# Four graph layers on 32 graphs: two broadcast sums moved from VectorE to GpSimd, one scaling moved from VectorE into ScalarE's PSUM evacuation

## The chip, the cores and the metric

The kernel runs on one core of one Trainium2 chip. The metric is device time in microseconds (us) of one execution; a run here is one such time. The engines are named as in the profile: PE (TensorE matmul) and PEld (its weight loads), DVE (VectorE), ACT (ScalarE), POOL (GpSimd), and SP (SyncE), whose queue issues all DMAs of this kernel.

## What is computed

Input is x of 32 graphs with 512 nodes and 256 features each, and adj, a 512 x 512 integer adjacency per graph. Four layers follow each other, each of the form

```
x = layernorm(x + layer(x, adj))
```

Layer 0 is graph attention with four heads of 64, a residual and a layernorm per head. Layer 1 is graph attention with a relu score and an elu. Layer 2 is a transformer block: eight heads of 32 over the symmetric adjacency, then a feed-forward of 1024. Layer 3, the one that the change touches most, is graph attention with one head:

```python
Wh = einsum('bnf,of->bno', h, W)
e = (Wh @ a1)[:, :, None] + (Wh @ a2)[:, None, :]
e = where(e > 0, e, 0.2 * e)
e = where(adj == 0, NEG_INF, e)
h_prime = einsum('bij,bjo->bio', softmax(e, axis=2), Wh)
```

## The kernel before

A graph's 512 nodes lie as R = 4 blocks of 128 rows on the partitions, so a tile of x is 128 x 4 x 256 fp32. K = 2 is the number of 128-wide pieces of the 256 features. Everything stays in SBUF from the load of a graph to its output.

**Exponentials without a score matrix.** In layers 0, 1 and 3 the exponential of a leaky relu of f + g is a maximum of two products. So the kernel takes exponentials of the two score columns alone (lines 665 to 667 in layer 3), brings one of them along the free axis with PE transposes into a bank gp and an ACT copy gb (line 345), and makes each masked weight tile pt with one DVE operation, max then multiply by the edges (line 393). What depends on the key alone, exp(0.2 g) in layer 3, is a factor on the key's row of values. In layer 3 it is written into column 256 of h (line 667) and multiplied onto the 256 value columns by DVE (line 668). The matmul of pt with 257 columns of h then gives numerators and the denominator at once.

**Projection.** `project` makes h from the transposed input: per row block two matmul steps into one PSUM bank, then one ACT copy of all columns into SBUF (line 333). Layers 0, 1 and 3 use it. In layer 3 the banks come from a pool of two that is shared with the feed-forward. Column 256 holds the query score f, column 257 the key score g.

**Two sums with a broadcast vector.** Layer 0 ends with a head layernorm scaled by gamma; its shift beta is added to the residual x earlier, off that path (line 437). In layer 2, `attended` makes y = x + bo for its own residual (line 599) and then adds the shift of the block's last layernorm to x (line 600), which is read again only at the end of the feed-forward (line 655). All three, 599, 600 and 437, are DVE operations on 128 x 1024 elements with the vector broadcast over the four row blocks.

**Layernorm.** `layernorm` takes statistics per row block on DVE (lines 266 and 267), adds eps (line 269), raises to the power -1/2 on POOL (line 270), multiplies by the mean (line 271) and applies scale and bias on ACT, one activation per row block (line 275). `head_layernorm` has a power on POOL of its own (line 297). Otherwise POOL sets a column of ones in layer 1 (line 466).

**Order of work.** The layers are generators; each yield carries a due time from the table PLACES plus PERIOD times the graph's number, and a merge by due time interleaves about three and a half graphs. PE's order is this merge, fixed by a manual schedule. On the other engines a scheduler of the tile framework sets the order when the program is built. Each engine runs its own queue in order and waits on semaphores.

At the end of each softmax part the row sums' reciprocals go to a tile rd, and a last check over them and over the adjacency decides whether a slower general program runs; with these inputs it does not.

## Time and profile before

| what | value |
|---|---|
| median of 3 runs | 3910.18 us (3910.09 to 3910.24) |
| profiled execution, its own time | 3906.41 us |
| its span, first to last instruction | 3904.6 us |
| mean granted TensorE clock | 0.983 |
| one graph in steady state | 116.77 us |
| DVE L437, 128 x 1024 | 1.22 us x32 |
| DVE L600, 128 x 1024 | 1.22 us x32 |
| DVE L668, 128 x 1024 | 1.22 us x32 |
| ACT L333 on h3p, 128 x 258 | 0.37 us x128 |

An engine's busy time is the sum over its instructions. Matmuls are pipelined and their ends are modelled. In a line of the timeline the numbers are start and length in us, then the engine, the line, the operation, output and inputs, and in brackets the idle time before it and what ended it. PE's matmuls all show line 102, so they are told apart by the tile that they write: h3p is layer 3's projection, gp the transposed exponentials, cp the attention of layer 2 times its values, xt1p and xt3p the transposed inputs of layers 1 and 3. L556 multiplies layer 2's exponentials pr by the edges.

### The profile page before, as it was taken

Reading aid. Unit: us, or ns where it says so; the run is one execution under the profiler, and the core shown is the slowest. Engines: PE = TensorE matmul, PEld = TensorE weight load, DVE = VectorE, ACT = ScalarE, POOL = GpSimd, SP = SyncE. Lnnn points to the kernel's source line nnn. Section 1 sums busy time; section 2 is a strip of 40 time slices with the busy share of each in tenths; the row PEclk is TensorE's granted clock in tenths of the full one; section 3 lists DMA queues with packets and bytes.
Section 4 is the critical chain, followed back from the end, with each engine's and each line's share of the span. In section 5 each row is a group of like instructions: output and inputs, shape, how many; then the busy total and the mean of one; then the engine's idle time right before and its main releaser. Section 6 shows DMA issues by size and latency. Waiting matters only on the chain.

```text
span 3904.6 us, 53602 instructions
## 1 busy us (share of the span) xinstructions
PE 3753.3 (96%) x19238; PEld 2824.5 (72%) x19238; DVE 2674.8 (69%) x5594; ACT 1926.2 (49%) x4257; POOL 346.9 (9%) x266
## 2 busy tenths in 40 slices
PE   5899999999999999999999999999999999999996
PEld 4577777777777777777777777777777777777764
DVE  4667676677677677677677677677777677777653
ACT  2444455444455544455544455545555544555442
POOL 0000010000010001010001010001010001010000
PEclk6899999999999999999999999999999999999998
DMA  3222222222222222222222222222222222221120
GB/s 106 77 73 65 72 58 67 71 76 67 70 60 65 71 76 69 68 62 63 71 76 71 66 63 64 69 76 71 66 65 65 65 76 74 63 67 58 49 54 12
DMA packets 180431, 261.20 MB, mean 67 GB/s; under 512 B 36800, under 2 KB 72768, under 8 KB 180160
## 3 DMA queue, kind: packets, MB, share of 16 engines
q1 hardware_dynamic: 180160, 257.71, 23.1%
q8 instruction: 155, 2.54, 0.3%
q14 instruction: 116, 0.95, 0.1%
HBM read 106.57 MB, written 16.78 MB: 32 GB/s over the span
## 4 chain that ended last, share of the span: by engine, by line
PE 60%; DVE 14%; issue 8%; ACT 5%; POOL 5%; POOLq 0%; ACTq 0%
PE o L102 16%; PE f1p L102 7%; PE f2p L102 6%; PE qkp L102 5%; PE cp L102 5%; DVE pr L556 4%; ACT y L275 4%; POOL rs L270 3%; PE h3p L102 3%; PE s L102 3%; PE h1p L102 3%; PE wop L102 3%; POOL st L297 2%; PE gp L102 2%; PE vp L102 2%
## 5 line engine op out<-in xcount | busy, mean ns | idle before, releaser
L556 DVE TENSOR_TENSOR pr<-pr,a 128x1024 f32<-128x1024 f32 x384 | 459.1, 1216 | 319.3 <-ACT pr L553 319.2
L275 ACT ACTIVATE y<-y,rs 128x256 f32<-128x256 f32 x768 | 398.4, 589 | 438.2 <-DVE rs L271 438.2
L393 DVE SCALAR_TENSOR_TENSOR pt<-gb,ex,at 128x512 f32<-128x512 f32 x768 | 530.6, 744 | 77.6 <-ACT gb L345 77.6
L553 ACT ACTIVATE pr<-s 128x512 f32<-128x512 f32 x1024 | 545.2, 613 | 7.4 <-PE s L102 7.3
L102 PEld LDWEIGHTS o<-hv,pt 128*128 128x128 f32 x4096 | 508.4, 199 | 23.7 <-issue 8.4
L102 PE MATMUL o<-hv,pt 128*128 128x65 f32 x4096 | 502.7, 280 | 9.7 <-DVE pt L393 9.7
L102 PE MATMUL f2p<-wf,ft 128*128 128x256 f32 x2048 | 491.6, 383 | 12.3 <-ACT ft L638 12.2
L102 PE MATMUL cp<-pr,v 128*64 128x512 f32 x2048 | 474.9, 600 | 17.8 <-DVE pr L556 17.1
L102 PE MATMUL f1p<-yt,wf 128*128 128x256 f32 x2048 | 488.9, 381 | 0.3 <-DVE yt L302 0.3
L102 PE MATMUL o<-h,pt 128*128 128x257 f32 x2048 | 482.8, 383 | 3.7 <-DVE pt L393 3.7
L102 PEld LDWEIGHTS o<-h,pt 128*128 128x128 f32 x2048 | 381.5, 190 | 96.0 <-issue 40.6
L270 POOL TENSOR_TENSOR rs<-rs,mhalf 128x4 f32<-128x4 f32 x192 | 246.2, 1282 | 2118.8 <-DVE rs L269 1826.0
L638 ACT ACTIVATE ft<-f1p,cols 128x256 f32<-128x256 f32 x512 | 215.2, 474 | 442.2 <-PE f1p L102 442.2
L102 PEld LDWEIGHTS f2p<-wf,ft 128*128 128x128 f32 x2048 | 380.1, 191 | 69.5 <-ACT ft L638 17.1
L102 PEld LDWEIGHTS f1p<-yt,wf 128*128 128x128 f32 x2048 | 385.3, 191 | 54.5 <-DVE yt L302 0.8
L102 PE MATMUL s<-qk 128*128 128x512 f32 x1024 | 395.1, 481 | 1.6 <-ACT pr L553 1.6
L102 PEld LDWEIGHTS cp<-pr,v 128*64 128x64 f32 x2048 | 133.0, 136 | 286.0 <-issue 194.2
L266 DVE BATCH_NORM_STATS2 bn<-y 128x6 f32<-128x256 f32 x768 | 294.6, 411 | 4.5
L102 PEld LDWEIGHTS s<-qk 128*128 128x128 f32 x1024 | 187.8, 190 | 99.3 <-issue 40.6
L102 PE MATMUL qkp<-xt,wqkv 128*128 128x512 f32 x512 | 231.3, 594 | 0.0
L345 ACT COPY gb<-gp 128x512 f32<-128x512 f32 x192 | 111.5, 581 | 219.4 <-PE gp L102 219.4
L428 DVE RECIPROCAL rd<-o 128x4 f32<-128x4 f32 x128 | 23.4, 183 | 272.7 <-PE o L102 272.7
(134 smaller groups left out, 4582.5 us busy)
## 6 DMA issues: line engine op xcount, KB each, us to landing
qk<-hi SPq DMA_DIRECT2D x1024, 64.0 KB, 2.0
qk<-lo SPq DMA_DIRECT2D x1024, 64.0 KB, 2.0
adjt<-in_adjt SPq DMA_DIRECT2D x64, 512.0 KB, 3.5
adj<-in_adj SPq DMA_DIRECT2D x64, 512.0 KB, 3.6
xt<-in_xt SPq DMA_DIRECT2D x32, 512.0 KB, 3.4
x<-in_x SPq DMA_DIRECT2D x32, 512.0 KB, 4.7
out<-y SPq DMA_DIRECT2D x32, 512.0 KB, 3.0
wf<-in_w1t SPq DMA_DIRECT2D x1, 1024.0 KB, 7.6
```

Of the source, the lines that this page charges most:

```text
L102: latest[0] = what(*args, **kwargs).ins.name
L266: nc.vector.bn_stats(st[:, r, :], y[:, r, :])
L270: nc.gpsimd.tensor_tensor(rs[:, 1, :], rs[:, 0, :], mhalf[:, :R], op=ALU.pow)
L275: nc.scalar.activation(y[:, r, :], y[:, r, :], AF.Identity, bias=rs[:, 2, r : r + 1], scale=rs[:, 1, r : r + 1],)
L297: nc.gpsimd.tensor_tensor(st[:, 2, :], st[:, 1, :], mhalf[:, :G], op=ALU.pow)
L345: nc.scalar.copy(g, p)
L393: nc.vector.scalar_tensor_tensor(t, g, f, edges, op0=ALU.max, op1=ALU.mult)
L428: nc.vector.reciprocal(rdh, o[:, :, HO:])
L553: nc.scalar.activation(t[:, i, :], s, AF.Exp, scale=QSCALE)
L556: nc.vector.tensor_mul(t, t, edges)
L638: nc.scalar.activation(ft[:, f, :], p[:, f, :], AF.Relu, bias=bf1[:, ff + f : ff + f + 1])
```

## The change

Three operations leave DVE. The sums of lines 437 and 600 are issued on POOL instead, with the same operands. The scaling of line 668 goes: `project` gets an optional slope, and for layer 3 each row block leaves PSUM in three ACT instructions instead of one: a copy of the two score columns, an exponential of the key score with scale 0.2 into a small tile f, and a scaled pass of the 256 value columns with f as the factor per partition.

```diff
-    def project(xt, w, cols, name):
+    def project(xt, w, cols, name, slope=None):
...
-            nc.scalar.copy(h[:, r, :], p[:, :cols])
+            if slope is None:
+                nc.scalar.copy(h[:, r, :], p[:, :cols])
+            else:
+                nc.scalar.copy(h[:, r, cols - 2 :], p[:, cols - 2 : cols])
+                f = buf([P, 1], "f", "f", 4)
+                nc.scalar.activation(f, p[:, cols - 1 : cols], AF.Exp, scale=slope)
+                nc.scalar.activation(h[:, r, : cols - 2], p[:, : cols - 2], AF.Identity, scale=f)
         return h
...
-        nc.vector.tensor_add(x, x, all_rows(bet0))
+        nc.gpsimd.tensor_add(x, x, all_rows(bet0))
...
-        nc.vector.tensor_add(x, x, all_rows(ln2b))
+        nc.gpsimd.tensor_add(x, x, all_rows(ln2b))
...
-        h = yield from project(xt, w3g, D + 2, "h3")
+        h = yield from project(xt, w3g, D + 2, "h3", 0.2)
...
-        nc.vector.tensor_mul(h[:, :, :D], h[:, :, :D], f.to_broadcast([P, R, D]))
```

In the built program PE's instructions keep their order. On POOL each graph's sum of line 600 stands directly behind the power of layer 0's closing layernorm of a later graph, and the sum of line 437 directly behind that. On ACT the scheduler places one of layer 3's exponentials (line 665) between the small pieces and the large piece of the last row block, and puts a layernorm's four passes (line 275) ahead of the first of layer 2's hi (line 504).

## The prediction

> **What bounds the kernel now.** The page's first part comes first:

> ```profile
> PE 3753.3 (96%) x19238; PEld 2824.5 (72%) x19238; DVE 2674.8 (69%) x5594; ACT 1926.2 (49%) x4257; POOL 346.9 (9%) x266
> ```

> TensorE is busy nearly always; the change takes nothing from it. The long pieces of the chain of waits repeat every 116.77 us (one graph), so I read one such stretch in the table of busy time by window:

> ```profile
> 1740.54:1857.30 116.76, 115.08 (x602) 86.94 (x601) 83.07 (x175) 60.02 (x133) 10.46 (x8) 1.00 0.24 69
> ```

> PE is busy 115.08 of 116.76 us at full clock, so all that any change off PE can win is 1.68 us a graph. PE's waits in that stretch (who waited for whom, total, times, longest):

> ```profile
> PE gp L102 <- ACT ex L665: 0.7, 1, 0.7
> PE xt3p L102 <- ACT y L275: 0.5, 3, 0.2
> PE cp L102 <- DVE pr L556: 0.5, 1, 0.5
> ```

> Two of these three places are touched. In the timeline of PE (start, length, work, idle before):

> ```profile
> 1794.46 1.94 PE L102 MATMUL cp<-pr,v 128*64 128x512 f32 x8
> 1796.89 1.94 PE L102 MATMUL cp<-pr,v 128*64 128x512 f32 x8 [0.49 <-DVE pr L556]
> ...
> 1844.78 2.01 PE L102 MATMUL h3p<-w3g,xt 128*128 128x258 f32 x8
> 1847.49 0.65 PE L102 MATMUL gp<-ident,ex 128*128 128x128 f32 x4 [0.70 <-ACT ex L665]
> ```

> DVE ahead of the first stall:

> ```profile
> 1793.45 1.19 DVE L599 TENSOR_TENSOR y<-y,bo_b 128x1024 f32<-128x1024 f32 x1
> 1795.54 0.16 DVE L271 SCALAR_TENSOR_TENSOR rs<-mv,rs 128x4 f32<-128x4 f32 x1 [0.90 <-POOL rs L270]
> 1795.62 1.22 DVE L556 TENSOR_TENSOR pr<-pr,a 128x1024 f32<-128x1024 f32 x1
> 1796.75 1.22 DVE L600 TENSOR_TENSOR y<-y,ln2b_b 128x1024 f32<-128x1024 f32 x1
> ```

> POOL there, and at a power of the same size with DVE idle:

> ```profile
> 1793.52 1.99 POOL L270 TENSOR_TENSOR rs<-rs,mhalf 128x4 f32<-128x4 f32 x1 [8.84 <-DVE rs L269]
> ...
> 1823.44 1.01 POOL L270 TENSOR_TENSOR rs<-rs,mhalf 128x4 f32<-128x4 f32 x1 [14.55 <-DVE rs L269]
> ```

> What to see: a DVE chain without slack, from layer 0's last output through L298, L440, L441, the statistics, the power on POOL (L270) and L271 to L556, ends in PE. L600 stands behind it and holds nobody. The power took 1.99 us instead of 1.01: it ended 0.87 us after L599 did (1794.64).

> ACT at the second stall:

> ```profile
> 1844.38 0.62 ACT L333 COPY h<-h3p 128x258 f32<-128x258 f32 x2
> 1844.89 0.58 ACT L345 COPY gb<-gp 128x512 f32<-128x512 f32 x1
> 1845.96 0.37 ACT L333 COPY h<-h3p 128x258 f32<-128x258 f32 x1 [0.48 <-PE h3p L102]
> 1846.83 0.37 ACT L333 COPY h<-h3p 128x258 f32<-128x258 f32 x1 [0.50 <-PE h3p L102]
> 1847.23 0.21 ACT L665 ACTIVATE ex<-h 128x4 f32<-128x4 f32 x1
> ```

> PE stands from the last h3p until the exponentials that gp transposes.

> [...] (1) [...] The trace agrees in one direction: powers that meet such a DVE operation end 0.87 us after it (L599 at 1794.64, power 1795.51; L384 at 1841.19, power 1842.06; L393 at 1858.87, power 1859.74). The other direction, DVE held by POOL, it does not show. (2) [...] The trace agrees at the start: memsets begin 0.06 us before the one ahead ends.

> **The change part by part.** The built order of PE's instructions is the same as before; DVE loses 96 instructions, POOL gains 64, ACT gains 256.

> *DVE's share.* L437, L600 and L668 leave DVE: 3 x 1.22 = 3.65 us a graph, 117 us in all. Worth nothing in time: at 1806.17 (L437) DVE next waits for ACT's softmax at 1809.34; L600 is followed by idle time until 1799.89; L668 (1849.43) lets layer 3's masks start 1.13 us sooner, but PE wants them at 1853.68 and did not wait. What covers this is PE's own work; without it, at the very end, L668 waited for by o3 saves below 0.1 us, since the gb copy ends then too (3885.69 against 3885.79).

> *L437 on POOL.* It waits for x's DMA: issued 1799.35, landing 4.7 us later, 1804.05. It then meets two L556 (1803.90 to 1806.26); whoever wins, all are done by 1808.7, and the next cp starts at 1811.21. Behind it on POOL stand the memset L466 (1808.79) and a power at 1823.44. Cost 0 (-0 to +0.5 a graph). Once, at 77.4 us, it follows a power directly: up to 2.3.

> *L600 on POOL.* In POOL's order it stands directly behind the power of 1793.52, ahead of L437. Its waits (L599, layer 1's output and its transposes) are over at 1794.64, so by (2) it starts with the power's end, 1795.5, as L271 is only being released (1795.54). L271 has two SBUF inputs, L556 too. [...] Its length is not in the trace: [...] and I take 2.3 with the handover (2.2 to 2.6). Then L271 starts at 1797.8, L556 ends 1799.1, and the second half of cp starts 2.3 us later; ACT's y (L275) and xt1p's transposes move with it (y ready 1800.1, PE there 1801.1: no more). PE's order is fixed and nothing after is ahead of PE, so the stall is not won back: **+2.3 us a graph** (0 if L271 wins, 2.6 at most). New waits for POOL in L441 and L655 come some 30 us after their sums: 0.

> *ACT's evacuation.* For each of four row blocks, one copy (0.37 us, next one 0.26 later) becomes a copy of 2 columns, an exponential of 1 and a scaled activation of 256, which waits for the exponential. Prices: [...] the exponential 0.19 (L667's row: 0.21 from SBUF); the scaled one 0.46 as L476. First block: 1844.38, 1844.45, 1844.67 to 1845.13, so its bank comes free 0.38 us later, and PE's third block starts at 1845.16. The second ends 1845.78, gb 1846.26 (its masks start 1846.46 on DVE: hidden). The third block is ready at 1846.31, its last piece ends 1847.09; the fourth at 1847.2: small copy to 1847.36, then, as the built order has it, L665's exponential ahead of the large piece, 1847.59. gp starts 1847.62 instead of 1847.49: **+0.13 us a graph** (-0.2 if the three pipeline, +0.5 if the exponential takes 0.3).

> *Reordering.* ACT now does a layernorm (four L275) ahead of the first hi (L504), 2.9 us later. SP's 32 copies for the first head pairs then start at 1745.9, not 1743.0, and end by 1769; the scores that need them come at 1775, and SP stands from 1770 to 1781.7 for PE anyway. Cost 0 (to +0.5).

> Sum: 2.3 + 0.13 = 2.43 us for the 30 graphs in which PE waits for L556 (30 times in the list of waits) = 73, plus 1 for the start: +74. The profiled execution has a span of 3904.6 and takes 3906.41; that becomes 3978.6 and 3980.4. It lies 3.8 below the median of the runs shown, so the median goes to 3984.

> **The rivals.**
> - *DVE wins the pair at 1795.5* (not slower): L271 and L556 get in first and L600 runs from 1796.84 to 1799.1, while DVE is idle until 1799.89. It decides if POOL's start comes over 0.05 us after the power's end, or if POOL does not hold DVE at all. For: only 0.03 us separate DVE from the power's end. [...] Then only 0.13 x 30 = +4: 3914 (3902 to 3925).
> - *Held in part*: accesses interleave and L556 stretches by 0.5 to 1.5 us: 3930 to 3960. The whole-instruction wait of the powers speaks against it.
> - *Both sums in a row*: x lands before 1797.8, DVE stands 4.6 us, +145: 4055. The landing at 1804 speaks against it.
> - *The evacuation gains*: ex after the small copy shortens PE's 0.70 by 0.2 or more, POOL hidden: -6 to -15, 3900.

> **How the numbers follow.** L600 holds DVE: 0.68 (3965 to 4006); DVE first: 0.15; in part: 0.08; both: 0.04; gain: 0.05. The range 3912 to 4006 takes in the first, the third and half of the second. 0.2% (7.8 us) is about what a measurement of this kernel can tell from no change. Faster: 0.05 and 0.02 of DVE first, 0.07; same: 0.10; slower: the rest, 0.83.

> **What would show it.** In the profile after: L600's sum on POOL starting as the power ends; L271 or L556 starting, or lasting, 2.3 us longer; PE's wait for L556 some 2.8 us a graph; a period of 119.2 us; gp's wait changed by 0.2 or less. Wrong if the period stays within 0.3 us of 116.77 or L600 starts after L556.

## The result: 2.2% slower, and the profile after

The changed kernel takes 3996.01 us (median of 4 runs, 3992.72 to 3997.44) against 3910.14 (4 runs, 3907.31 to 3910.24): a ratio of 1.022, with an interval of 1.0203 to 1.0238, or +86 us where +74 was forecast. Its profiled execution took 3997.44 us, with a span of 3995.7 (before 3906.41 and 3904.6) and a mean granted clock of 0.979 (before 0.983).

Numbers of lines in the profile after: up to about line 332 one more than before (L270 is L271, L271 is L272), later seven more (L437 is L444, L556 is L563, L600 is L607, L665 is L672). The new ones are L337 (copy of two columns), L339 (exponential) and L340 (scaled pass).

The first part of the page:

```profile
PE 3770.8 (94%) x19144; PEld 2829.4 (71%) x19238; DVE 2684.7 (67%) x5498; ACT 1961.9 (49%) x4513; POOL 513.3 (13%) x330
```

DVE lost 96 instructions, 117 us of work, and is busy for 9.9 us more than before. So some of its instructions last longer. (Where two instructions of an engine overlap, its busy time counts that time once, so it is not simply the sum over them.) PE's busy time grew by 17.5 us, and the span by 91.1: the other 73.6 us are new idle time of PE. Which matmuls it stands before is in the groups of instructions (busy time and mean ns, then idle time just before them and what ended it). f2p is the feed-forward's second product, and ft, which ACT makes, is what it multiplies. The first line is cp's of the profile before, the rest is of the profile after:

```profile
L102 PE MATMUL cp<-pr,v 128*64 128x512 f32 x2048 | 474.9, 600 | 17.8 <-DVE pr L556 17.1 <-DVE mv L267 0.6
```

```profile
L103 PE MATMUL cp<-pr,v 128*64 128x512 f32 x2048 | 483.9, 610 | 81.5 <-DVE pr L563 80.8 <-DVE mv L268 0.6
L103 PE MATMUL f2p<-wf,ft 128*128 128x256 f32 x2048 | 491.1, 383 | 18.2 <-ACT ft L645 18.1
L103 PE MATMUL h3p<-w3g,xt 128*128 128x258 f32 x512 | 132.3, 391 | 8.6 <-ACT h L340 8.6
L103 PE MATMUL gp<-ident,ex 128*128 128x128 f32 x768 | 119.4, 279 | 18.6 <-ACT ex L672 15.7 <-ACT ex L471 1.3 <-ACT ex L415 0.8
```

Before, these four stood at 17.8, 12.3, 0.3 and 25.7 us. So cp takes 63.7 of the 73.6 us, f2p 5.9, h3p 8.3, gp gives back 7.1, and smaller groups have the other 2.8. The wait for layer 2's masked exponentials is most of the new idle time, and 63.7 of the 91.1 us of the span; it is the wait that the prediction named.

One graph in steady state, by the table of busy time by window (length; busy us of PE, PEld, DVE, ACT and POOL with counts; granted clock; DMA share; GB/s):

```profile
1427.10:1546.29 119.19, 115.23 (x599) 86.96 (x601) 84.12 (x172) 61.07 (x141) 16.28 (x11) 1.00 0.24 67
1068.20:1188.72 120.52, 116.56 (x598) 87.24 (x601) 83.01 (x172) 61.26 (x141) 15.43 (x11) 0.99 0.23 66
```

Four graphs of five are like the first line: 119.19 us against 116.77, and forecast was 119.2. The fifth takes 1.4 us more, and the added time is PE's busy time at a lower granted clock. PE's waits in the first stretch (in total, times, longest):

```profile
PE cp L103 <- DVE pr L563: 2.7, 1, 2.7
PE gp L103 <- ACT ex L672: 0.5, 1, 0.5
PE xt3p L103 <- ACT y L276: 0.5, 3, 0.2
PE h3p L103 <- ACT h L340: 0.2, 1, 0.2
```

The first wait grew from 0.5 to 2.7 us, gp's shrank from 0.7 to 0.5, and h3p's is new. What stood ahead of the first wait is in the timeline of POOL and in that of DVE (start, length, work, idle before):

```profile
1480.19 1.99 POOL L271 TENSOR_TENSOR rs<-rs,mhalf 128x4 f32<-128x4 f32 x1 [8.84 <-DVE rs L270]
1482.15 2.34 POOL L607 TENSOR_TENSOR y<-y,ln2b_b 128x1024 f32<-128x1024 f32 x1
1492.96 3.19 POOL L444 TENSOR_TENSOR x<-x,bet_b 128x1024 f32<-128x1024 f32 x1 [8.47 <-DMA x<-in_x]
```

```profile
1480.12 1.19 DVE L606 TENSOR_TENSOR y<-y,bo_b 128x1024 f32<-128x1024 f32 x1
1482.21 2.30 DVE L272 SCALAR_TENSOR_TENSOR rs<-mv,rs 128x4 f32<-128x4 f32 x1 [0.90 <-POOL rs L271]
1484.43 1.21 DVE L563 TENSOR_TENSOR pr<-pr,a 128x1024 f32<-128x1024 f32 x1
...
1492.70 4.52 DVE L563 TENSOR_TENSOR pr<-pr,a 128x1024 f32<-128x1024 f32 x2 [3.32 <-ACT pr L560]
```

What to see: POOL's sum follows the power without a gap and runs to 1484.49. DVE's L272, a multiplication of 128 x 4 elements that took 0.16 us before, is released at 1482.21 and lasts until 1484.51, as long as the sum does. Only then L563 runs, and PE's second half of cp follows it at 1485.70. The profile shows the time for which L272 is held as its length (2.30 us), not as idle time before it (0.90). So the stall is not found in any list of DVE's waits; it shows as a mean of 485 ns where 163 was, for L272's 192 instructions:

```profile
L272 DVE SCALAR_TENSOR_TENSOR rs<-mv,rs 128x4 f32<-128x4 f32 x192 | 93.2, 485 | 183.1 <-POOL rs L271 183.1
```

The last line of DVE's timeline is the same thing again with the other sum: two L563 take 4.52 us where 2.36 would be usual, while L444 runs. PE was busy with other work there, and nothing was lost.

Not every DVE operation is held beside the sum. In the first graph L607 runs at another place, beside DVE operations that read the transposed output of layer 2's attention (ctp) from PSUM. L594 has that input alone, L598 one more from SBUF. They start and end inside the sum, at the length that they have elsewhere (medians 0.19 and 0.42 us). POOL and DVE there:

```profile
195.83 2.37 POOL L607 TENSOR_TENSOR y<-y,ln2b_b 128x1024 f32<-128x1024 f32 x1 [16.20 <-PE o L103]
```

```profile
196.74 0.20 DVE L594 RECIPROCAL rd<-ctp 128x8 f32<-128x8 f32 x1
196.97 0.42 DVE L598 TENSOR_TENSOR ctx<-ctp,rd 128x256 f32<-128x256 f32 x1
```

The two that the sums held, L272 (2.30 us for 0.16) and L563 (4.52 us for 2.36), take both inputs from SBUF.

At the second place, ACT's timeline for the last row block of layer 3:

```profile
1536.01 0.16 ACT L337 COPY h<-h3p 128x2 f32<-128x2 f32 x1
1536.07 0.18 ACT L339 ACTIVATE f<-h3p 128x1 f32<-128x1 f32 x1
1536.20 0.21 ACT L672 ACTIVATE ex<-h 128x4 f32<-128x4 f32 x1
1536.32 0.46 ACT L340 ACTIVATE h<-h3p,f 128x256 f32<-128x256 f32 x1
```

and PE's (wop is layer 2's output projection):

```profile
1532.69 1.03 PE L103 MATMUL wop<-wo,ct 128*128 128x256 f32 x4
1533.96 2.01 PE L103 MATMUL h3p<-w3g,xt 128*128 128x258 f32 x8 [0.24 <-ACT h L340]
1536.46 0.65 PE L103 MATMUL gp<-ident,ex 128*128 128x128 f32 x4 [0.49 <-ACT ex L672]
```

From wop to gp PE now takes 3.77 us where it took 3.62 (1843.87 to 1847.49 before). The new break before h3p shows only 0.24 us of idle time, yet gp's wait is 0.21 shorter and the stretch is 0.15 longer. Without a break, in the profile before, h3p starts 0.12 us before wop's modelled end (1844.78 against 1844.90); with the break that overlap is lost too.

### The profile page after: what moved, and what is told of

Same layout as the page of the kernel before. It is cut to its first block, busy times and chain, and to the rows that moved or that the text cites. A ratio compares the mean times of both kernels' runs of the same rounds, so it can differ in the third digit from the quotient of the medians.

```text
span 3995.7 us, 54011 instructions
## 1 busy us (share of the span) xinstructions
PE 3770.8 (94%) x19144; PEld 2829.4 (71%) x19238; DVE 2684.7 (67%) x5498; ACT 1961.9 (49%) x4513; POOL 513.3 (13%) x330
## 4 chain that ended last, share of the span: by engine, by line
PE 52%; DVE 27%; ACT 8%; POOL 7%; issue 2%; DVEq 0%; POOLq 0%; ACTq 0%
PE o L103 16%; PE f2p L103 6%; PE f1p L103 6%; DVE pr L563 6%; PE qkp L103 5%; ACT y L276 5%; PE cp L103 5%; POOL rs L271 4%; DVE bn L267 4%; PE h1p L103 3%; PE s L103 3%; POOL st L298 2%; DVE rs L272 2%; PE gp L103 2%; PE h3p L103 2%
## 5 line engine op out<-in xcount | busy, mean ns | idle before, releaser
L563 DVE TENSOR_TENSOR pr<-pr,a 128x1024 f32<-128x1024 f32 x384 | 510.7, 1350 | 303.8 <-ACT pr L560 303.8
L103 PE MATMUL cp<-pr,v 128*64 128x512 f32 x2048 | 483.9, 610 | 81.5 <-DVE pr L563 80.8
L271 POOL TENSOR_TENSOR rs<-rs,mhalf 128x4 f32<-128x4 f32 x192 | 246.9, 1286 | 2066.3 <-DVE rs L270 1788.5
L103 PEld LDWEIGHTS f2p<-wf,ft 128*128 128x128 f32 x2048 | 380.2, 191 | 73.6 <-ACT ft L645 23.5
L298 POOL TENSOR_TENSOR st<-st,mhalf 128x16 f32<-128x16 f32 x32 | 95.6, 2986 | 991.7 <-DVE st L297 991.7
L272 DVE SCALAR_TENSOR_TENSOR rs<-mv,rs 128x4 f32<-128x4 f32 x192 | 93.2, 485 | 183.1 <-POOL rs L271 183.1
```

Source lines behind the costliest of these rows:

```text
L103: latest[0] = what(*args, **kwargs).ins.name
L271: nc.gpsimd.tensor_tensor(rs[:, 1, :], rs[:, 0, :], mhalf[:, :R], op=ALU.pow)
L272: nc.vector.scalar_tensor_tensor(rs[:, 2, :], mv[:, :, 0], -1.0, rs[:, 1, :], op0=ALU.mult, op1=ALU.mult)
L298: nc.gpsimd.tensor_tensor(st[:, 2, :], st[:, 1, :], mhalf[:, :G], op=ALU.pow)
L563: nc.vector.tensor_mul(t, t, edges)
```

## The experiments

Two theories stood at first. **Held**: POOL's sum, standing directly behind the power, holds L271 and L556 for its whole length, and this is nearly all of the loss. **Elsewhere**: the loss comes from the evacuation, from the other sum, or from the new order of ACT and POOL, and the sum of line 600 is a bystander. The kernel before ran at 3909.81, 3909.78 and 3910.06 us beside the three groups of runs; ratios are to that, with 95% intervals. Except for longpow, split3 and best, the first time expected of a kernel is that of Held.

### u600: the change without the sum of line 600 on POOL

```diff
-        nc.gpsimd.tensor_add(x, x, all_rows(ln2b))
+        nc.vector.tensor_add(x, x, all_rows(ln2b))
```

> The changed kernel with the sum of line 600 back on DVE. [...] (the whole loss is L600's POOL add holding L271 and L556 once a graph): 3914 us (3906 to 3922), PE's wait for L556 back to 0.5 us a graph, period 116.9. Evacuation theory (the three ACT pieces, or the new order on ACT, cost the time): stays at 3985 or more. Any-POOL-add theory (each of the two sums costs about half): about 3953.

Measured: 3925.75 us, ratio 1.0041 (1.0026 to 1.0055). A graph takes 117.04 us and PE's wait for L563 is 0.6 us. Of the +86 us, 70 go with this one line. The 16 us that stay are more than was expected, 3925.75 being above the range; onlyevac below has most of them.

### only600: the kernel before with that sum alone on POOL

```diff
-        nc.vector.tensor_add(x, x, all_rows(ln2b))
+        nc.gpsimd.tensor_add(x, x, all_rows(ln2b))
```

> The kernel before with only the sum of line 600 on POOL. [...] 3990 us (3978 to 3998), L271 on DVE lasting about 2.3 us behind the power, period 119.0. Evacuation theory: 3912. Any-POOL-add theory: about 3950.

Measured: 3989.01 us, 1.0201 (1.0184 to 1.0218). DVE's timeline:

```profile
1591.96 2.30 DVE L271 SCALAR_TENSOR_TENSOR rs<-mv,rs 128x4 f32<-128x4 f32 x1 [0.90 <-POOL rs L270]
1594.19 1.21 DVE L556 TENSOR_TENSOR pr<-pr,a 128x1024 f32<-128x1024 f32 x1
```

The line alone brings +79 us, with the same 2.30 us in the same place, and PE's wait there is 2.6 us. A graph takes 118.93 us, every third one 120.52.

### only437: the kernel before with the sum of line 437 alone on POOL

```diff
-        nc.vector.tensor_add(x, x, all_rows(bet0))
+        nc.gpsimd.tensor_add(x, x, all_rows(bet0))
```

> The kernel before with only the sum of line 437 on POOL. [...] in which the place decides: 3911 us (3906 to 3918), although the add meets two DVE multiplications L556 and one of them is stretched or waits. Any-POOL-add theory: about 3950.

Measured: 3914.55 us, 1.0011 (1.0002 to 1.0019). A graph takes 116.80 us, 0.03 more than before: in steady state the sum is free. What it costs it costs once, at the start, where it stands directly behind a power. POOL and DVE there:

```profile
76.85 1.01 POOL L270 TENSOR_TENSOR rs<-rs,mhalf 128x4 f32<-128x4 f32 x1 [7.79 <-DVE rs L269]
77.83 2.34 POOL L437 TENSOR_TENSOR x<-x,bet_b 128x1024 f32<-128x1024 f32 x1
```

```profile
77.89 2.29 DVE L271 SCALAR_TENSOR_TENSOR rs<-mv,rs 128x4 f32<-128x4 f32 x1 [1.12 <-POOL rs L270]
```

PE's first wait for layer 1's input grows from 19.7 to 21.8 us by it. In the changed kernel the same sum waited there for its DMA, 0.16 us past the power's end, and that wait of PE is 19.6: L272 went first. Its DVE line, and POOL's two:

```profile
79.09 0.16 DVE L272 SCALAR_TENSOR_TENSOR rs<-mv,rs 128x4 f32<-128x4 f32 x1 [1.12 <-POOL rs L271]
```

```profile
78.05 1.01 POOL L271 TENSOR_TENSOR rs<-rs,mhalf 128x4 f32<-128x4 f32 x1 [7.79 <-DVE rs L270]
79.22 2.35 POOL L444 TENSOR_TENSOR x<-x,bet_b 128x1024 f32<-128x1024 f32 x1 [0.16 <-DMA x<-in_x]
```

In these two traces the sum that starts with the power's end is ahead of DVE by 0.06 us, and L271 lasts 2.29 us; the one that starts 0.16 us after it is not, and L272 lasts 0.16. The rest of the +4.7 us of the median, beyond 2.1 at the start and 0.03 a graph, is within the interval.

### onlyevac: the kernel before with the new evacuation alone

```diff
...
-            nc.scalar.copy(h[:, r, :], p[:, :cols])
+            if slope is None:
+                nc.scalar.copy(h[:, r, :], p[:, :cols])
+            else:
...
+                nc.scalar.activation(h[:, r, : cols - 2], p[:, : cols - 2], AF.Identity, scale=f)
...
-        nc.vector.tensor_mul(h[:, :, :D], h[:, :, :D], f.to_broadcast([P, R, D]))
```

> The kernel before with only the scaled evacuation of layer 3. [...] 3915 us (3908 to 3922): 0.15 us a graph on PE, as the wait of gp falls from 0.7 to 0.5 and a wait of 0.24 for the bank appears. Evacuation theory: 3985 or more.

Measured: 3923.13 us, 1.0032 (1.0019 to 1.0044): +13, more than the +4 of the forecast's steps, and just above the range expected. A graph takes 117.05 us, +0.28, of which 0.15 is the stretch from wop to gp above and 0.1 is the wait for L563, 0.6 instead of 0.5. That is 28 x 0.28 = 8 us. The rest fell in once: the third period is 122.61 us against 117.70. PE's waits between 340 and 480 us, and ACT's timeline there:

```profile
PE f2p L103 <- ACT ft L645: 3.8, 1, 3.8
```

```profile
392.66 0.47 ACT L645 ACTIVATE ft<-f1p,cols 128x256 f32<-128x256 f32 x1 [0.35 <-PE f1p L103]
396.16 2.08 ACT L276 ACTIVATE y<-y,rs 128x256 f32<-128x256 f32 x4 [3.02 <-DVE rs L272]
398.14 0.45 ACT L645 ACTIVATE ft<-f1p,cols 128x256 f32<-128x256 f32 x1
```

In this one graph ACT's order has the four passes of a layernorm between two passes of the feed-forward (ft). They wait for DVE, the second ft waits behind them, and PE waits for it. In the kernel before, both ft come first (388.37, two together, and the layernorm at 394.38), and PE has no such wait. It is the scheduler's new order that costs here, not an instruction's length.

### memset: does any POOL instruction hold DVE?

The changed kernel, with two memsets of x in place of the sum of line 600, so that x's part in layer 2's output is left out.

```diff
-        nc.gpsimd.tensor_add(x, x, all_rows(ln2b))
+        nc.gpsimd.memset(x, 0.0)
+        nc.gpsimd.memset(x, 0.0)
```

> The changed kernel with the sum of line 600 on POOL replaced by two memsets of the same tile, some 1 us each, that wait for the same and stand in the same place of POOL's queue; x's part in layer 2's output is left out. [...] L271 stays at 0.16 us and the kernel is at 3914 us (3906 to 3924). Queue theory (the power's completion, or DVE, is held because POOL is busy with what is behind it, read or not): about 3975.

Measured: 3921.11 us, 1.003 (1.0019 to 1.0042). POOL and DVE in the same place:

```profile
1575.06 0.94 POOL L607 MEMSET y<- 128x1024 f32 x1
1576.07 0.95 POOL L608 MEMSET y<- 128x1024 f32 x1
```

```profile
1575.14 0.16 DVE L272 SCALAR_TENSOR_TENSOR rs<-mv,rs 128x4 f32<-128x4 f32 x1 [0.90 <-POOL rs L271]
1575.22 1.22 DVE L563 TENSOR_TENSOR pr<-pr,a 128x1024 f32<-128x1024 f32 x1
```

POOL stands where the sum stood and is busy for 1.96 us, and DVE passes beside it as if it were not there. L272 takes 0.16 us here and 2.30 beside the sum. So it is not POOL's being busy, nor its queue, that holds DVE here. The sum reads two inputs from SBUF and the memset reads nothing; that the reading is what holds DVE was not shown by itself. Together with the operations on ctp above (0.20 and 0.42 us, not held), this bounds what was seen: DVE operations with both inputs in SBUF, held by POOL sums that read SBUF.

### halves: the sum of line 600 in two

The changed kernel with two POOL sums of 512 elements each.

```diff
-        nc.gpsimd.tensor_add(x, x, all_rows(ln2b))
+        for i in range(0, R, 2):
+            nc.gpsimd.tensor_add(
+                x[:, i : i + 2, :], x[:, i : i + 2, :], ln2b.unsqueeze(1).to_broadcast([P, 2, D])
+            )
```

> The changed kernel with the sum of line 600 cut into two POOL adds of 512 elements. [...] L271 waits for the first half (1.2 us); then either DVE gets in between (its L271, perhaps L556, then the second half): 1.2 to 1.6 us a graph, 3952 to 3965 us; or the second half is ahead too: 3996. [...] 3996, as nothing changes in their sum.

Measured: 3958.07 us, 1.0125 (1.0108 to 1.0141); a graph takes 118.12 us and PE's wait for L563 is 1.7. POOL and DVE:

```profile
1587.99 3.55 POOL L608 TENSOR_TENSOR y<-y,ln2b_b 128x512 f32<-128x512 f32 x2
```

```profile
1588.05 1.22 DVE L272 SCALAR_TENSOR_TENSOR rs<-mv,rs 128x4 f32<-128x4 f32 x1 [0.90 <-POOL rs L271]
1589.19 1.21 DVE L563 TENSOR_TENSOR pr<-pr,a 128x1024 f32<-128x1024 f32 x1
```

L272 stands for one half only, and then L563 passes as well: POOL's pair takes 3.55 us, about 1.2 more than the 2.34 of the whole sum, and 1.2 is L563's length. So between the halves the waiting DVE goes ahead of POOL's second sum, and the hold here is 1.22 us, as long as one of POOL's two instructions and not as long as both.

### later600: the same sum on POOL, in another place

The changed kernel, with the sum bound into POOL's order in the feed-forward, at a point where DVE has no two-input operation waiting.

```diff
-        nc.gpsimd.tensor_add(x, x, all_rows(ln2b))
...
+                if r == 0 and ff == 2:
+                    in_place(nc.gpsimd.tensor_add(x, x, all_rows(ln2b)))
```

> The changed kernel with the sum of line 600 still on POOL, tied to a place in the feed-forward (row block 0, third pair of hidden blocks), where DVE stands idle for PE for over 5 us. [...] in which the place decides and not the move: 3914 us (3906 to 3922), no DVE operation stretched by it. If the add costs wherever it stands: 3985 or more.

Measured: 3925.94 us, 1.0043 (1.0026 to 1.006), above the range expected as u600 is, and the time of u600 (3925.75), where DVE does the sum. On POOL in this place it costs nothing, and that DVE does not have to do it gains nothing. The place decides, not the engine.

### longpow: a pause of the same length without any sum on POOL

The kernel before, with a power of 12 elements whose result is not used ahead of layer 0's closing power. It lets L271 wait longer for POOL; all sums stay on DVE. It is there to separate the hold from the pause that it causes.

```diff
...
+        if idle:
+            more = buf([P, 16], "more", "more", 2)
+            nc.gpsimd.tensor_tensor(
+                more[:, :idle], rs[:, 0, :1].to_broadcast([P, idle]), mhalf[:, :idle], op=ALU.pow
+            )
         nc.gpsimd.tensor_tensor(rs[:, 1, :], rs[:, 0, :], mhalf[:, :R], op=ALU.pow)
...
-        layernorm(y, 1e-5)
+        layernorm(y, 1e-5, 12)
```

> The kernel before with a second, unused power of 12 elements on POOL ahead of the power of layer 0's closing layernorm; no sum moves. It makes PE's wait for L556 as long as in the changed kernel (about 2.7 us) by a plain wait of L271 for POOL, with DVE free [...]. If the extra 1.4 us that some graphs of the changed kernel take come from the length of PE's pause: the same extra in every third to fifth graph, 3984 us (3976 to 3992). [...] none of it, all periods equal near 119.0, 3976.

Measured: 3999.9 us, 1.023 (1.0215 to 1.0246). PE's wait is 2.7 us as in the changed kernel. Two graphs in the table of busy time by window:

```profile
1189.00:1308.00 119.00, 115.09 (x601) 86.97 (x601) 83.08 (x176) 60.00 (x133) 12.98 (x9) 1.00 0.24 67
1308.00:1428.40 120.40, 116.47 (x601) 87.25 (x601) 83.09 (x176) 60.19 (x133) 12.98 (x9) 0.99 0.24 66
```

Every third graph takes 1.4 us more, with more busy time of PE and a lower granted clock, as every fifth does in the changed kernel. So these 1.4 us come with PE's pause of 2.7 us and not from a POOL sum's hold on DVE, which is not there. The time is above the range expected because the start grew too, by 3.5 us, the first three periods by 5.8, 4.9 and 3.9, and the last by 1.9; I have not traced which wait each of these is.

### move599 and split3: what the profile of before offered

The power of line 270 takes 1.99 us beside L599 and 1.01 with DVE idle. move599 is the kernel before, with line 599's sum bound into DVE's order behind the second cp, from the second graph on. The new `with_bo` makes y = x + bo, and binds it where it stands if its second argument is true.

```diff
...
+            if hp == 1 and early:
+                y = with_bo(x, True)
...
-        y = sb.tile([P, R, D], F32, tag="y2", name="y2", bufs=2)
-        nc.vector.tensor_add(y, x, all_rows(bo))
+        y = y or with_bo(x, False)
```

> The kernel before, all sums on DVE, with the sum of line 599 (y = x + bo) tied behind the second cp instead of standing between L269 and L271 (from the second graph on). [...] L599 holds the power for 1 us now and DVE itself for 1.2; without it the power takes 1.0 us and L556 ends before PE wants it, so the wait of 0.5 us a graph goes: 3896 us (3890 to 3904). If the wait is set elsewhere: 3910.

Measured: 3898.45 us, 0.9971 (0.996 to 0.9982); a graph takes 116.37 us. The power:

```profile
1559.49 1.01 POOL L270 TENSOR_TENSOR rs<-rs,mhalf 128x4 f32<-128x4 f32 x1 [8.84 <-DVE rs L269]
```

PE's wait for layer 2's product with the edges is gone from its list.

split3 is the kernel before, with the last row block of layer 3 alone cut: its two score columns first, then the exponential that gp needs, then the 256 values (`scores` issues line 665's exponential). The scaling stays on DVE.

```diff
...
+            if scores and r == R - 1:
+                nc.scalar.copy(h[:, r, D:cols], p[:, D:cols])
+                done = scores(h).ins.name
+                rest = nc.scalar.copy(h[:, r, :D], p[:, :D])
+                tc.add_manual_dep(rest.ins, done, ALL, reason="after the scores")
...
```

> The kernel before with only the last of layer 3's four row blocks split on ACT: its two score columns first, then the exponential that gp transposes (line 665), then the 256 values; line 668 stays on DVE and no sum moves. If gp's wait ends with that exponential and nothing else: it falls from 0.7 to about 0.4 us a graph, 3902 us (3896 to 3907). If the exponential only trades its wait with another (the bank, or DVE's L668): 3910.

Measured: 3903.54 us, 0.9983 (0.9975 to 0.9991); gp's wait falls from 0.7 to 0.5 us, and a graph takes 116.57. The gain that the changed evacuation has at gp is had here without its loss at h3p.

### best: both, with the sum of line 600 on POOL in its harmless place

The kernel before with the edits of move599 and split3 and, of the change under study, line 600's sum on POOL where later600 puts it.

> All three together: the sum of line 599 tied behind the second cp (DVE), the sum of line 600 on POOL in the feed-forward's idle stretch of DVE, the last row block of layer 3 split as in the run before; the sum of line 437 and the scaling stay on DVE. Place theory: gains add up, 3890 us (3882 to 3897), since L600 on POOL costs nothing there. If any POOL add of this size costs: 3905 or more.

Measured: 3893.6 us, 0.9955 (0.9942 to 0.9969), faster than both kernels; a graph takes 116.18 us, with PE busy for 115.20 of them.

## Why the prediction was right, and where its sum was short

*DVE's relief is worth nothing*: right. later600 and u600 differ by 0.2 us, though DVE has 39 us less to do in one.

*L600 on POOL*: right in place and in size. It starts with the power's end, L271 stands for 2.30 us against 2.3 taken, and the sum lasts 2.34. PE's wait grew by 2.2 us. That the sum would hold L271 and L556, and for how long, was the author's estimate: the trace of before shows only powers held by DVE (1.99 us for 1.01) and no sum on POOL. DVE held by POOL was the largest risk in the forecast; only600 shows it (2.30 us), and memset (0.16 us) and the operations on ctp (0.20 and 0.42 us) bound it.

*L437 on POOL*: right in steady state, 0.03 us a graph. It does hold DVE, by 2.2 us at 1492.70, under cover of PE's work. The once-only cost at the start shows in only437, but not in the changed kernel.

*The evacuation*: its prices hold (the exponential 0.176 and the scaled pass 0.470 us in the groups after, against 0.19 and 0.46; the small copy, which no trace had priced, took 0.153), and so does the step at gp, +0.15 against +0.13. It was short by the 0.1 us of the wait for L563, which onlyevac, u600 and later600 all show; what moves that wait is not traced.

*Reordering, "Cost 0 (to +0.5)"*: wrong. I followed one move of ACT's order in steady state and took it for all of them. In the third period ACT has a layernorm ahead of an ft that PE wants. Alone that cost PE 3.8 us (onlyevac); in the changed kernel, with L272 held by the sum in the same chain, it cost 5.9:

```profile
PE f2p L103 <- ACT ft L645: 5.9, 1, 5.9
```

*The sum.* +74 was forecast; +86 was measured on the medians, +91.1 on the spans of the two profiled executions. Its wait at cp was sized about right: 2.74 us against 0.49 in each of 28 graphs and 63.7 in all, where 2.3 x 30 = 69 was taken. That all of PE's new idle time, 73.6 us, comes to the 74 of the forecast is luck: the ft wait, put at nothing, and the waits at h3p and gp fill up what cp has less.

The term that is missing is PE's own busy time, which the forecast left as it was, at full clock: it grew by 17.5 us. 9.0 of these are in cp's own group (483.9 against 474.9 us), and that is the clock: after seven of the pauses the second cp ran at half the clock, with a graph some 1.4 us longer each time. About 4 are overlap lost at h3p's new break, 0.12 us a graph. 2.4 lie in the first 340 us, where move599 and split3 too have 2.8 and 3.4 us more than the profile of before, so they are not put down to the change. Some 2 us stay open.

*The rivals*: "DVE wins the pair" fell in steady state, since L607 starts 0.06 us ahead of L272; the point that it named is real, though (L444 at 79.22 us, above); "held in part" fell, since the hold is as long as the sum in only600 (2.30 us) and as long as the first half in halves (1.22 us); "both sums in a row" did not occur (L444 at 1492.96, 8.47 us after L607's end; its +145 is also 2 more than 4.6 x 30 + 4 + 1); "the evacuation gains" has its mechanism in split3, but in the change h3p's wait takes the gain back.

The parts do not add up: only600, only437 and onlyevac sum to 79 + 5 + 13 = 97, and together they cost 86. In the changed kernel L437's hold at the start does not occur (2 us), and the cp at half the clock comes every fifth graph, in only600 every third: 7 times against 11, some 6 us. The rest is within the intervals.

## What to carry to other kernels

Before moving an elementwise operation to GpSimd, look at what stands next in both queues: with SBUF inputs it can hold DVE's operations on two SBUF inputs for its whole length, as it did here, and a DVE multiplication of four elements a partition, 0.16 us otherwise, then takes as long (2.30 us) as the sum (2.34). If it must go there, bind it to a place where DVE is idle, or cut it so that the hold is short (1.22 us in halves); the relief of an engine that the end does not wait for is worth nothing by itself. Look for such holds in the mean length of small instructions, not in the waits, and read the built order of the first graphs as well as of a steady one.

## What the runs showed of the hardware that was not expected

```profile
1126.79 3.29 PE L103 MATMUL cp<-pr,v 128*64 128x512 f32 x8 [2.75 <-DVE pr L563]
```

and the windows of 1 us around it (the granted clock stands third from the end):

```profile
1125.00:1126.00 1.00, 0.00 (x0) 0.00 (x0) 1.00 (x2) 0.37 (x1) 0.58 (x1) 1.00 0.44 109
1126.00:1127.00 1.00, 0.21 (x2) 0.22 (x4) 0.73 (x1) 1.00 (x3) 0.00 (x0) 0.57 0.00 0
1127.00:1128.00 1.00, 1.00 (x4) 0.32 (x4) 0.00 (x0) 1.00 (x3) 0.00 (x0) 0.50 0.00 0
1128.00:1129.00 1.00, 1.00 (x4) 0.24 (x2) 0.00 (x0) 1.00 (x3) 0.00 (x0) 0.50 0.00 0
1129.00:1130.00 1.00, 1.00 (x4) 0.00 (x0) 0.00 (x0) 0.47 (x2) 0.00 (x0) 0.73 0.11 31
```

The clock is half (0.50) for about 3.4 us, from late in the pause on, and the cp takes 3.29 us instead of 1.94.

The grid is in the traces' records of the granted clock. In the traces after, only600, longpow and halves every change of the clock lies within 0.001 us of one grid of 3.4133 us, from the first graph to the last. The rhythm of the slow graphs agrees: the five graphs from one such cp to the next take 4 x 119.19 + 120.55 = 597.3 us, or 175.0 windows of the grid; the three of only600 take 2 x 118.93 + 120.52 = 358.4, and those of longpow 2 x 119.00 + 120.41 = 358.4, both 105.0 windows.

Cut PE's timeline on that grid, from 660 to 3650 us: in after, only600 and longpow the clock was halved 21 times, each time in the window that follows one in which PE stood for 2.10 to 2.48 us, and it stayed full after every window in which PE stood for 1.96 us or less. No window there lies between. So in these runs the same pause of 2.7 us cost 1.4 us more where one window held at least 2.1 us of it, and nothing more where the edge of a window left less than 2.0 us on either side. The pause of 1.7 us in halves gave no window more than 1.68 us, and brought no slow graph. At the start and at the end of the execution the clock also falls after windows with less idle time than this (in after, at 211.36 us after one with 0.46 us, at 3795.36 after one with 1.45); why is open.
